# A Mamba scan kernel: the carried state of slot 10 joined one slot ahead, the first dt loaded in slot 27, the gate z copied one half a slot

## The chip, the cores and the metric

The kernel runs on one core of one Trainium2 chip. The metric is the device time of one execution in microseconds (us). Three runs of the kernel before gave 4239.77, 4239.93 and 4242.26 us; the median, 4239.93 us, is the time before.

## The reference, cut to what matters

The program computes two layers of a hybrid of convolution, attention and Mamba on 4096 tokens of 256 channels, and then a mixture of two experts. The change lies in the Mamba stage alone. That stage computes, for each of two directions (forward, and backward over the reversed tokens):

```
xc, z = split(in_proj(x));  xc = silu(conv4(xc));  dt, B, C = x_proj(xc);  dt = softplus(dt_proj(dt))
h[t] = exp(dt[t] * A) * h[t-1] + dt[t] * B[t] * xc[t]        # 512 channels x 16 states
y[t] = sum over states (h[t] * C[t]) + xc[t] * Dp;   out = out_proj(y * silu(z))
```

Both directions are added, normalised, put through a small two-layer network and added to the input.

## The kernel before, in words

Four stages follow each other: convolutions with depthwise taps, attention, the Mamba stage (mamba_phase), and the experts. All tensors are float32.

The Mamba stage works in 16 chunks, numbered i: 8 blocks of 512 tokens, with the two directions taken in turn (d = i % 2). A chunk has 4 channel groups e, 4 state groups k and 2 halves j of a group: 32 slots, numbered at = 8 e + 2 k + j/2. One slot is one scan instruction on VectorE (DVE) over 128 lanes and 2 x 512 elements. A lane is a pair of channel and state, and two runs of 512 tokens stand side by side in one instruction. For a slot n these steps exist, each of them on a fixed engine:

- decay(n), ScalarE (ACT), line L1667: two exponentials that make the factors da in PSUM. Two such PSUM tiles exist.
- inflow(n), GpSimd (POOL), L1677: the product dbx of the loaded row dtxr with the row b. Three dbx tiles exist.
- bring(n), ACT, L1708: adds the state carried over from the chunk before into the first element of the second run, in dbx. It exists from chunk 2 on, and it needs inflow(n) and the tile brought.
- recur(n), DVE: the scan, L1688, and in 27 of 32 slots the product with the row c, L1693. In slots 4, 10, 12, 18 and 28 (POOLED) that product is made by POOL, L1698.
- keep(n), ACT, L1716: stores the end of the scan as the state.
- sum_states, TensorE (PE), L1723 and L1725: sums over states into y. close (DVE, L1733) multiplies y with the gate z.

The order of the instructions on each engine is the order of the loop body; each engine runs its own list in that order and waits where a value is missing. In slot n the body issues: carry (if this slot has one), inflow(n+2), keep(n-1), decay(n+1), bring(n+1), recur(n), the loads for later slots, sum_states, and then one step of each generator that runs beside the scan: prepare (the projections, convolution and dt of chunk i+1), from slot 27 on also the prepare of chunk i+2, and tail (the small network of a finished block), whose pieces are held back in slots where the named engine is full.

The steps of prepare(q) fall into fixed slots of chunk q-1: the Silu of xc (L1301, with a load of ACT's function table ahead of it and another behind it, for the next exponential) in slot 8, the projection by wx (PE, L1306) in slot 9, the Ln (L1346) in slot 23, and the last six steps in slots 24 to 29. In those six, dt_piece adds the softplus on POOL (L1370), takes the first dt of every row (L1375) and writes it to DRAM (first_row, L1378, by the SP queue, one for each pair of channel groups), or writes the dt rows themselves (dtd, L1385). load_first (L1391, SP) reads first_row back, spread over the 128 lanes, as first_r. The z part (L1251 on PE, two products at a time in the two PSUM tiles "mm"; L1362 on ACT, the copies into z) lies there too.

The tile brought is made by carry in three parts: POOL multiplies first_r with A (L1401), ACT takes the exponential (L1403), and POOL multiplies with the old state (L1406). For channel groups 0 and 1 of the next chunk (h = 0) part 0 is issued at the start of slot 30, part 1 at the end of slot 30, part 2 at the start of slot 31. For groups 2 and 3 (h = 1) this is done in slots 9, 10 and 11 of the chunk itself, with load_first in slot 1.

All loads and stores of the stage go through one queue, SP, in the order of the code: besides the above the rows b and c (L1414), dtr and dtxr (L1424; the two for slots 0 and 1 are issued in slots 27 and 29 of the chunk before), and u (L1260). An SP instruction that must wait holds everything behind it. Its transfers take eight completion semaphores in turn.

Of the kernel before, what the change touches and what calls it, by code (L numbers as in the profile page):

```python
# [14 lines left out]
FP = mybir.dt.float32  # L15
# [9 lines left out]
P = 128  # L25
# [4 lines left out]
N = 512  # L30
# [1137 lines left out]
def mamba_phase(cx, early, w_in, w_x, w_out, w1, w2, x1d, ud, bcd, dtd, x2d, u2d, usum):  # L1168
# [11 lines left out]
    nc, tc = cx.nc, cx.tc  # L1180
    with ExitStack() as ctx:
# [87 lines left out]
        def prepare(q):  # L1269

            d, got = q % 2, gots[q]

            ps = in_pair(q, 0)
            yield
            yield
            xp = early.wide("xp")
            nc.scalar.copy(xp[:, :, 0:3], halo[d])
            for v in range(2):
                nc.scalar.copy(xp[:, v, 3:], ps[v])
            ps = in_pair(q, 2)  # L1280
            yield
            yield
            for v in range(2):
                nc.scalar.copy(xp[:, 2 + v, 3:], ps[v])
            nc.scalar.copy(halo[d], xp[:, :, N : N + 3])
            for _ in range(4):
                yield

            xc = None
            for e in range(ET + 1):  # L1290
                if e > 0:
                    xc = got["xc"] = xc or pr.tile([P, ET, N], FP, name="xc", tag="xc")
                    nc.scalar.activation(xc[:, e - 1, :], ps, AF.Identity, bias=cx.col(f"convb{d}", e - 1))
                if e < ET:
                    ps = mm_psum()
                    for k in range(4):
                        nc.tensor.matmul(  # L1297
                            ps, taps[d][:, 4 * e + k, :], xp[:, e, k : k + N], start=k == 0, stop=k == 3
                        )
                yield  # L1300
            nc.scalar.activation(xc, xc, AF.Silu)  # L1301
            yield
            ps = mm_psum()
            nx = DR + 2 * DS
            for e in range(ET):
                nc.tensor.matmul(ps[0:nx, :], wx[d][:, e, :], xc[:, e, :], start=e == 0, stop=e == ET - 1)  # L1306
            yield
            xd = few()[0:nx, :]
            nc.scalar.copy(xd, ps[0:nx, :])

            at = 0 if d else DR
            nc.sync.dma_start(out=bcd[q], in_=xd[at : at + 2 * DS, :])
            yield


            r = slice(32 * d, 32 * d + DR)
            ex = dt = None
            for e in range(ET + 1):
                if e > 0:
                    ex = early.wide("ex")[:, :, 0:N] if e == 1 else ex  # L1320
                    dt = dt or sp.tile([P, ET, N], FP, name="dt", tag="dt")
                    nc.scalar.activation(ex[:, e - 1, :], ps, AF.Abs, bias=cx.col(f"dtb{d}", e - 1))
                    nc.scalar.activation(dt[:, e - 1, :], ps, AF.Relu, bias=cx.col(f"dtb{d}", e - 1))
                if e < ET:
                    ps = mm_psum()
                    nc.tensor.matmul(ps, wdt[r, P * e : P * e + P], xd[r, :], start=True, stop=True)
                yield

            nc.scalar.activation(ex, ex, AF.Exp, scale=-1.0)
            yield  # L1330
            rds, sums = {}, {}
            for e in range(ET + 2):
                if e < ET:
                    rd = rds[e] = few()
                    nc.scalar.activation(rd, ex[:, e, :], AF.Identity, scale=-1.0, bias=-1.0)
                    nc.scalar.add(rd, rd, 1.0)
                if e > 1:
                    nc.scalar.copy(dt[:, e - 2, :], sums.pop(e - 2))
                if 0 < e <= ET:
                    ps = sums[e - 1] = mm_psum()  # L1340
                    for v, x in enumerate((rds.pop(e - 1), ex[:, e - 1, :], dt[:, e - 1, :])):
                        nc.tensor.matmul(ps, cx.ident, x, start=v == 0, stop=v == 2)
                yield


            nc.scalar.activation(ex, ex, AF.Ln, bias=1.0)  # L1346
            zs = in_pair(q, ET)
            yield
            got["dt"] = dt
            for at, (v, e) in enumerate(((0, 0), (1, 0), (0, 1), (0, 2), (0, 3), (1, 1))):  # L1350
                dt_piece(q, v, e, ex)
                if at == 4 and q > 1:
                    load_first(q, 0)
                if at == 1:
                    zs = in_pair(q, ET + 2)
                    if q + 1 < 2 * NCH:
                        load_u(q + 1)
                if at in (0, 2):
                    z = sp.tile([P, 2, N], FP, name="z", tag="z", bufs=3)
                    got.setdefault("z", []).append(z)  # L1360
                    for f in range(2):
                        nc.scalar.copy(z[:, f, :], zs[f])  # L1362
                yield

        def dt_piece(q, v, e, ex=None, eng=nc.gpsimd):
# [387 lines left out]
        with tc.manual_schedule(engines=ORDERED):  # L1753
            gots[0] = {"u": early.u}
            begin = start()
            step(begin)
            coming = prepare(1)
            tails, prep, out, ending = [], None, None, None
            for n, (i, e, k, j) in enumerate(slots):
                at = n % SPS  # L1760
                if at == 0:
                    prep, coming = coming, None
                if at in CARRY and 1 < i + (at > 16) < 2 * NCH:
                    carry(i + (at > 16), *CARRY[at])
                inflow(n + 2)
                if n > 0:
                    keep(n - 1)
                if n > 0:
                    decay(n + 1)
                bring(n + 1)  # L1770
                if at == 8:
                    bring(n + 2)
                recur(n)
                nxt = (i, e + 1) if e < ET - 1 else (i + 1, 0)
                if nxt[0] < 2 * NCH:
                    if e == ET - 1 and j == 0:
                        load_bc(i + 1, k)
                    if (k, j) == (1, 2):
                        load_dt(*nxt, 0)
                    if (k, j) == (2, 2):  # L1780
                        load_dt(*nxt, 2)
                if n > 0 and (n - 1) % SPS in POOLED:
                    pooled(n - 1)
                if j == 2 and n > 2 and (n - 3) % SPS in POOLED:
                    sum_states(n - 3)
                if j == 0 and n > 0:
                    if (n - 2) % SPS not in POOLED:
                        sum_states(n - 2)
                    if k == 0:
                        close(*slots[n - 2][:2])  # L1790
                        if e == 0:
                            out = output(i - 1)
                if 1 <= at <= 3 and out is not None:
                    step(out)
                    if at == 3:
                        out = None
                        if (i - 1) % 2:
                            tails.append(tail((i - 1) // 2))
                if at == 0 and i > 0:
                    for z in gots[i]["z"]:  # L1800
                        nc.scalar.activation(z, z, AF.Silu)
                if i == 0:
                    step(begin)
                step(prep, LATE.get(at, 1) if i == 0 else 1)
                if at >= SPS - AHEAD and i + 2 < 2 * NCH:
                    coming = coming or prepare(i + 2)
                    step(coming)
                if i > 0 and at in (2, 4):
                    dt_piece(i, 1, 2 if at == 2 else 3)
                if at == 1 and i > 1:  # L1810
                    load_first(i, 1)
                elif at in (10, 30) and 1 < i + (at > 16) < 2 * NCH:
                    carry(i + (at > 16), at < 16, 1)
                if i == 2 * NCH - 1 and at in (26, 28):
                    ending = ending or last_output()
                    step(ending)
                if tails and (i == 2 * NCH - 1 or at not in FULL[needs[0]]):
                    needs[0] = next(tails[0], None)
                    if needs[0] is None:
                        tails.pop(0)  # L1820
                        needs[0] = "PE"
            sum_states(len(slots) - 2)
            close(2 * NCH - 1, ET - 1)
            for t in tails:
                drain(t)
            drain(ending)
            last_tail(NCH - 1)
# [324 lines left out]
```

## Time and profile before

| what | value |
|---|---|
| median of three runs | 4239.93 us |
| the profiled execution: its own time | 4233.11 us |
| its span, first to last instruction | 4231.3 us |
| convolutions and attention, start of span to 2016 us: DVE busy | 1644.6 of 2016 us |
| Mamba, chunks 0 and 1, 2016 to 2254 us: DVE busy | 216.8 of 238 us |
| Mamba, chunks 2 to 15, 2254 to 3910 us: DVE, ACT, POOL, PE busy | 1575.1, 1267.0, 1422.4, 1342.1 of 1656 us |
| end of Mamba and experts, 3910 to 4231 us: PE busy | 278.3 of 321 us |
| granted TensorE clock, share of full | 0.918 |

A row of the groups names the line, the engine, the operation, the tiles written and read, the count, the busy time and mean duration, and after the second bar the idle time just before such instructions with what ended it. A row of the waits names who waited for whom, the time in total, how often, and the longest. A row of the timeline names the start, the duration, the engine, the line, and in brackets the idle time before. In the tables of waits a wait is put down to the semaphore that came last by the profile, so a name can be that of a neighbour on the same engine.

### The profile page before, as it was taken

The page shows a single profiled execution, that of the slowest core. Times are in us where ns is not written, and L with a number is a line of the kernel's source. Part 1 is how long each engine was busy: PE and PEld are TensorE (multiplying, and loading weights), DVE is VectorE, ACT ScalarE, POOL GpSimd, SP SyncE. Part 2 cuts the span into 40 slices and gives each one's busy share as a digit, 9 for nine tenths or more (in the row PEclk, how much of TensorE's full clock was granted, in tenths as well). Part 3 has the DMA queues.
Part 4 walks back from the last instruction along what each step waited for, and adds up shares of the span by engine and source line. Part 5 has one row for each costly group of instructions (what it writes and reads, how often), then busy time and mean ns, then how long its engine had stood idle before and what let it go on. Part 6 is the DMA issues. An engine that isn't in the chain of part 4 may idle for free. (4 is left out here: it accounts for less than half of the span.)

```text
span 4231.3 us, 43479 instructions
## 1 busy us (share of the span) xinstructions
PE 3603.2 (85%) x15080; PEld 1175.6 (28%) x15080; DVE 3503.0 (83%) x2898; ACT 2675.6 (63%) x4176; POOL 1740.9 (41%) x1132
## 2 busy tenths in 40 slices
PE   4769894999999999999788888878888888875798
PEld 2324341222222222222222222222222222321343
DVE  6997876888888888778899999999999999999211
ACT  1111224888788788777777778777787777774122
POOL 2210000000000000000888889888888888897000
PEclk9889996999999999999888999989899898977899
DMA  4422224000000000002333443433334433432121
GB/s 160 138 77 92 75 75 133 4 28 15 21 26 11 24 24 15 17 14 74 115 125 113 130 117 123 126 115 123 115 108 125 130 124 116 133 117 73 65 65 39
DMA packets 150531, 351.18 MB, mean 83 GB/s; under 512 B 35493, under 2 KB 44453, under 8 KB 150046
## 3 DMA queue, kind: packets, MB, share of 16 engines
q1 hardware_dynamic: 139214, 313.17, 23.4%
q0 software_dynamic: 11088, 35.14, 2.4%
q8 instruction: 120, 1.97, 0.2%
q14 instruction: 109, 0.89, 0.1%
HBM read 268.69 MB, written 79.56 MB: 82 GB/s over the span
## 5 line engine op out<-in xcount | busy, mean ns | idle before, releaser
L1677 POOL TENSOR_TENSOR dbx<-dtxr,b 128x1024 f32<-128x1024 f32 x512 | 1203.0, 2361 | 201.9 <-DVE da L1688 106.0
L961 ACT ACTIVATE e<-sc 128x1024 f32<-128x1024 f32 x1024 | 992.6, 1023 | 201.4 <-PE sc L954 160.3
L1688 DVE TENSOR_TENSOR_SCAN da<-da,state,dbx 128x1024 f32<-128x1024 f32 x432 | 1014.3, 2348 | 40.4 <-ACT state L1716 19.3
L882 DVE TENSOR_TENSOR s<-s,e 128x1024 f32<-128x1024 f32 x768 | 880.8, 1218 | 45.4 <-ACT e L961 44.9
L1667 ACT ACTIVATE da<-dtr,aneg 128x512 f32<-128x512 f32 x1024 | 708.0, 691 | 32.8 <-DMA dtr<-dtd 2.9
L954 PE MATMUL sc<-q,kS 32*128 32x512 f32 x4096 | 653.6, 643 | 19.5 <-DMA kS<-kd 13.0
L132 POOL TENSOR_TENSOR ln_few<-ln_few,minus_half 128x4 f32<-128x4 f32 x29 | 29.5, 1016 | 1414.2 <-DMA ln_few<-ln_row 1414.2
L1693 DVE TENSOR_TENSOR h<-da,c 128x1024 f32<-128x1024 f32 x432 | 529.2, 1225 | 32.6 <-DVE da L1688 0.4
L889 PE MATMUL av<-e,vT 128*32 128x512 f32 x4096 | 548.9, 607 | 3.7 <-ACT o L895 3.7
L452 PE MATMUL cv<-v,u 128*128 128x512 f32 x928 | 420.7, 614 | 58.8 <-DVE pad L272 21.2
L1725 PE MATMUL y<-h,sel 128*32 128x512 f32 x2048 | 378.7, 655 | 101.3 <-DVE h L1693 83.9
L954 PEld LDWEIGHTS sc<-q,kS 32*128 32x128 f32 x4096 | 211.6, 183 | 465.5 <-issue 244.3
L1251 PE MATMUL mm<-u,win 128*128 128x512 f32 x496 | 255.4, 663 | 80.9 <-ACT z L1362 34.3
L452 PEld LDWEIGHTS cv<-v,u 128*128 128x128 f32 x928 | 181.1, 197 | 294.6 <-issue 241.3
L528 DVE SCALAR_TENSOR_TENSOR acc<-pad,wdw_s,acc 128x768 f32<-128x768 f32 (+1 forms) x192 | 244.6, 1279 | 19.0 <-ACT acc L524 13.3
L1716 ACT COPY state<-da 128x2 f32<-128x2 f32 x431 | 68.1, 158 | 257.9 <-DVE h L1693 256.8
L1297 PE MATMUL mm<-xp,taps 128*128 128x512 f32 x480 | 213.6, 597 | 3.5 <-DVE m L1446 3.4
L882 DVE TENSOR_TENSOR s<-e 128x1024 f32<-128x1024 f32 x128 | 150.9, 1220 | 72.8 <-ACT e L961 72.6
L1688 DVE TENSOR_TENSOR_SCAN h<-da,state,dbx 128x1024 f32<-128x1024 f32 x80 | 187.5, 2343 | 16.5 <-ACT state L1716 7.0
L889 PEld LDWEIGHTS av<-e,vT 128*32 128x32 f32 x4096 | 81.3, 108 | 395.9 <-issue 378.3
L1698 POOL TENSOR_TENSOR h<-h,c 128x1024 f32<-128x1024 f32 x80 | 188.6, 2358 | 2.1 <-ACT state L1716 2.1
L1251 PEld LDWEIGHTS mm<-u,win 128*128 128x128 f32 x496 | 100.9, 212 | 236.5 <-issue 105.1
(347 smaller groups left out, 3821.3 us busy)
## 6 DMA issues: line engine op xcount, KB each, us to landing
dtr<-dtd SPq DMA_DIRECT2D x128, 512.0 KB
dtxr<-dtd SPq DMA_DIRECT2D x128, 512.0 KB
b<-bcd SPq DMA_DIRECT2D x64, 256.0 KB
c<-bcd SPq DMA_DIRECT2D x64, 256.0 KB
dtd<-dt SPq DMA_DIRECT2D x64, 256.0 KB
dtd<-few SPq DMA_DIRECT2D x64, 256.0 KB
u<-uv SPq DMA_DIRECT2D x24, 640.0 KB
u<-ud SPq DMA_DIRECT2D x16, 512.0 KB
```

The source lines that it names most:

```text
L452: nc.tensor.matmul(rows4(ps), u[:, dy, P * ci : P * ci + P], v[:, dy : dy + HR, ci, :], start=dy + ci == 0, stop=dy == k - 1 and ci == CT - 1,
L528: nc.vector.scalar_tensor_tensor(o, src, w_ap, o, ALU.mult, ALU.add)
L882: nc.vector.tensor_tensor(z, x, y, ALU.add)
L889: nc.tensor.matmul(g.av[32 * h : 32 * h + 32, :], vT[:, kb, P * t + 32 * h : P * t + 32 * h + 32], es[h // 2][:, h % 2, :], start=kb == 0, ...
L954: nc.tensor.matmul(ps[h // 2][:, h % 2, :], kS[r, t, P * kb : P * kb + P], q_t[r, t, :], start=True, stop=True,)
L961: nc.scalar.activation(e, ps[i], AF.Exp)
L1251: nc.tensor.matmul(ps, win[d][:, t, P * e : P * e + P], u[:, t, ::-1] if d else u[:, t, :], start=t == 0, stop=t == CT - 1,)
L1667: nc.scalar.activation(da[:, v, :], dts[i, e, j][0][:, v, :], AF.Exp, scale=aneg[i % 2][:, a : a + 1])
L1677: nc.gpsimd.tensor_tensor(u, dts[i, e, j][1], bcs[i, k][0][:, None, :].to_broadcast([P, 2, N]), ALU.mult)
L1688: nc.vector.tensor_tensor_scan(das[n].rearrange("p v n -> p (v n)"), da.rearrange("p v n -> p (v n)"), u.rearrange("p v n -> p (v n)"), st ...
L1693: nc.vector.tensor_tensor(h, da, bcs[i, k][1][:, None, :].to_broadcast([P, 2, N]), ALU.mult)
L1725: nc.tensor.matmul(ys[i, e][32 * j : 32 * j + 32, :], cx.sel, hs[n + j // 2][:, j % 2, :], start=False, stop=k == SQ - 1,)
```

## The change

In slot 8 the body issued bring(9) and, at once behind it, bring(10); it now issues bring(9) alone, and bring(10) follows decay(10) in slot 9 as for every other slot. load_first(q, 0) moves from behind dt_piece(q, 0, 3) in slot 28 to ahead of dt_piece(q, 0, 2) in slot 27. The four z copies, made two at a time in slots 24 and 26, are now made one each in slots 24, 25, 26 and 27; the one in slot 25 stands ahead of the second pair of z projections. No instruction is added or dropped. The orders of POOL, PE and DVE stay as they were.

```diff
             for at, (v, e) in enumerate(((0, 0), (1, 0), (0, 1), (0, 2), (0, 3), (1, 1))):
+                if at == 3 and q > 1:
+                    load_first(q, 0)
                 dt_piece(q, v, e, ex)
-                if at == 4 and q > 1:
-                    load_first(q, 0)
+                if at in (0, 2):
+                    z = sp.tile([P, 2, N], FP, name="z", tag="z", bufs=3)
+                    got.setdefault("z", []).append(z)
+                if at < 4:
+                    nc.scalar.copy(z[:, at % 2, :], zs[at % 2])
                 if at == 1:
                     zs = in_pair(q, ET + 2)
                     if q + 1 < 2 * NCH:
                         load_u(q + 1)
-                if at in (0, 2):
-                    z = sp.tile([P, 2, N], FP, name="z", tag="z", bufs=3)
-                    got.setdefault("z", []).append(z)
-                    for f in range(2):
-                        nc.scalar.copy(z[:, f, :], zs[f])
                 yield
...
                 bring(n + 1)
-                if at == 8:
-                    bring(n + 2)
                 recur(n)
```

## The prediction

> **What bounds the kernel now.** I read the stages' busy times first: only Mamba is touched, and in chunks 2 to 15 DVE is busy 1575 of 1656 us (95%). The groups then say what DVE does there, and the waits say who stops it.
>
> ```profile
> L1688 DVE TENSOR_TENSOR_SCAN da<-da,state,dbx 128x1024 f32<-128x1024 f32 x432 | 1014.3, 2348 | 40.4 <-ACT state L1716 19.3
> ```
>
> With the product of L1693 (1.23 us, below) a slot costs 3.58 us of DVE. The change touches none of that, so it can only win or lose DVE's idle time. The waits of DVE in chunks 2 to 15, then those of ACT:
>
> ```profile
> DVE da L1688 <- ACT state L1716: 17.7, 21, 2.0
> DVE da L1688 <- ACT dbx L1708: 12.7, 15, 3.1
> ```
> ```profile
> ACT brought L1403 <- POOL brought L1401: 29.6, 13, 4.5
> ACT dbx L1708 <- POOL dbx L1677: 20.9, 21, 2.0
> ```
>
> DVE waits for ACT, and ACT waits for POOL at just the instructions that the change moves. By slot (the scans of the timeline numbered 0 to 511; a stall is the idle time before a scan over the -0.08 us that scans show back to back) the stalls of over 0.1 us in chunks 2 to 15 lie at slot 0 (9.8 us in sum), slot 2 (15.6), slot 10 (16.2), 25 (2.9) and 26 (3.9), with a few single ones at slots 12 and 13; all other scans follow without a gap.
>
> Slot 10 in chunk 5, ACT's timeline, then DVE's:
>
> ```profile
> 2638.08 0.28 ACT L1708 ACTIVATE dbx<-dbx,brought 128x1 f32<-128x1 f32 x1
> 2639.15 0.29 ACT L1708 ACTIVATE dbx<-dbx,brought 128x1 f32<-128x1 f32 x1 [0.79 <-POOL dbx L1677]
> 2639.45 1.28 ACT L1301 ACT_TABLE_LOAD   x1
> 2640.74 1.91 ACT L1301 ACTIVATE xc<-xc 128x2048 f32<-128x2048 f32 x1
> ...
> 2644.01 1.42 ACT L1667 ACTIVATE da<-dtr,aneg 128x512 f32<-128x512 f32 x2
> ```
> ```profile
> 2642.99 1.23 DVE L1693 TENSOR_TENSOR h<-da,c 128x1024 f32<-128x1024 f32 x1
> 2645.53 2.35 DVE L1688 TENSOR_TENSOR_SCAN h<-da,state,dbx 128x1024 f32<-128x1024 f32 x1 [1.32 <-ACT da L1667]
> ```
>
> ACT stands idle for inflow(10); behind that wait are queued Silu and both table loads, then decay(10), which ends 0.10 us before scan 10 starts. That wait is on the path.
>
> [...] The trace has 16 landing marks for a first_row, up to 4.7 us from first to last. [...] load_first must wait on SP for the last mark of first_row. In the trace, first_r into chunk 2 is issued 0.07 us after that mark.
>
> **bring(10).** In slot 8 it costs ACT its wait (0.79 us in chunk 5) and 0.28 us. In slot 9, inflow(10) is long done (2639.11), so it costs 0.28 us behind decay(10), of which 0.14 shows (decay end to scan is 0.24 us where a bring stands between, 0.10 here). Nothing else holds Silu: its input is ACT's own, and keep(8) and decay(10) need DVE results of 2638.76 and 2640.09. So scan 10 gains the smaller of its stall and wait + 0.14. Waits of ACT by chunk: 0.66, 1.52, 0.79, 1.52, 0.41, 1.50, 1.44, 1.51, 0.75, 2.01, 0.87, 1.51 in chunks 3 to 14; in 2 and 15 none, and no stall. Stalls: 1.27, 1.00, 1.40, 1.00, 1.16, 1.33, 2.05, 0.99, 1.35, 2.12, 1.48, 1.00. Sum of the smaller ones: 13.2 us. What is late next? wx on PE follows Silu and comes earlier too; inflow(13) has over 2 us. I take -13.0; the ends are -9 (0.3 us lost in each) and -16 (all stalls).
>
> **First dt.** SP into chunk 6, and the POOL step that needs it:
>
> ```profile
> 2709.00 0.55 SPq L1378 DMA_DIRECT2D first_row<-first  x1
> ...
> 2710.86 0.60 SPq L1414 DMA_DIRECT2D b<-bcd  x1
> 2713.31 0.51 SPq L1414 DMA_DIRECT2D c<-bcd  x1
> 2715.91 0.33 SPq L1378 DMA_DIRECT2D first_row<-first  x1
> 2716.33 0.72 SPq L1391 DMA_DIRECT2D first_r<-first_row  x1
> ```
> ```profile
> 2723.56 0.22 POOL L1401 TENSOR_TENSOR brought<-aneg,first_r 128x16 f32<-128x16 f32 x1 [1.57 <-DMA dtxr<-dtd]
> ```
>
> The releaser named is a neighbour: first_r's last mark is at 2723.49. The new place is behind the first dtxr, issued at 2710.26 in this list, but first_row lands at 2715.17, so the issue is near 2715.2, 1.1 us earlier; what counts is that b and c, 512 KB, then lie behind it: I expect the landing near dtxr's, 2718.5. POOL is ready at 2721.99, so the whole wait on L1401 goes, in 8 of 14 boundaries by over 0.1 us (3.35, 2.73, 1.37, 0.24, 1.57, 2.71, 1.90, 2.37). Slot 0's stall goes with it. But slot 2 of the next chunk is late next: its bring(1) needs inflow(1), and that needs the second dtxr, whose landing (2725.95) is set by the same transfers, only reordered. From bring(1) to scan 2 are 6.6 us of Silu, two table loads and decay. With x for the shift of that landing, scan 2 gains, into chunks 2 to 7, 11 and 13: 0.93, 0.96, 0.04, 0.05, 0.80, 0.71, 0.25, 0.32, each less x; 4.1 us at x = 0, and chunk 14 loses x as well: 9x. Behind SP's new wait stand b, c, first_row and dtr/dtxr, issued up to 1.2 us later than now (into chunk 4), though that still is over 7 us ahead of their landing. The trace doesn't show this order. Ends for x: -0.5 (fewer early loads compete) and 1.2 us (the issue delay shows fully); I take 0.3[...]. So -4.1 + 2.7 = -1.4; ends -8 and +6.5.
>
> **z.** In the seven even chunks from 2 on scan 26 stalls 0.55 us behind this ACT queue:
>
> ```profile
> 2583.03 1.05 ACT L1362 COPY z<-mm 128x512 f32<-128x512 f32 x2
> 2583.97 1.52 ACT L1457 ACTIVATE hn<-hn,small 128x512 f32<-128x512 f32 x2
> ...
> 2585.57 1.42 ACT L1667 ACTIVATE da<-dtr,aneg 128x512 f32<-128x512 f32 x2
> ```
>
> One copy fewer ahead (1.05 - 0.57 = 0.48 us) ends it: 7 x 0.48 = 3.4 us. The added wait is PE's: the second product of slot 25 waits for the copy behind bring(26), up to 0.4 us, with u's load behind it on SP and all of the above behind that. Where the landing sets slot 2 the 0.48 is lost again, which leaves about two of seven: -1.0; ends -3.8 and +2. In odd chunks bring(26) has over 4 us before scan 26: nothing, covered by scan 25 and a tail step.
>
> **Sum.** -13.0 - 1.4 - 1.0 = -15.4 us. Against the profiled execution: 4233.1 - 15.4 = 4217.7. That execution lay 6.8 us under the median of the runs; on the median, 4239.9 - 15.4 = 4224.5.
>
> **Rivals.** (1) Given back: slot 10 gains, but x is 1.2 and PE's wait costs 2 us: -13 + 6.5 + 2 = -4.5, 4235.4. For it: DVE-bound stretches end at slot 2, where the landing decides; against it: the landings come over 7 us after issue. (2) Slower: SP, blocked on first_row, leaves the DMA engines dry, so that the second dtxr lands 3 us later. Then nine boundaries lose 27 - 4 and the others, whose slack is 0.9 to 3.5 us, some 5 more: +28 - 13 = +15, 4254.9. It decides from x = 1.8 on. For it: first_row lands 6 to 8 us after its issue in the busy boundaries. Against: dtr and dtxr, 1 MB, are still moving when first_row lands. (3) No effect: what is freed at slot 10 is waited for at slots 11 to 13, by PE's wx or POOL: 4239. For it: chunk 15 stalls 1.1 us at slot 12. Against: ACT's whole queue moves up with Silu, so its exponential and POOL's part 2 do too.
>
> **Chances.** Forecast 0.70 (4216 to 4231), rival 1 0.17, rival 2 0.08, rival 3 0.05. A difference under 0.2% (8.5 us) can't be told from none: rivals 1 and 3 lie within. Of the forecast 0.02 ends there too, and of rival 1 0.06 passes 4231.5: faster 0.74, same 0.18, slower 0.08. The range, 4215 to 4238, leaves out rival 2, part of 3, and a gain of over 25 us.
>
> **What would show it.** Right: ACT has no idle time ahead of Silu in slot 8, scan 10's stalls sum to about 3 us, L1403's wait for L1401 falls from 29.6 to under 18, scan 0 hardly stalls. Slot 2's stalls grow, from 15.6 towards 15.6 + 9.8 - 1.4 = 24 us, since slot 0's move there; slot 26's vanish. Wrong: L1677's wait for dtxr at slot 1 grows by more than 1 us a boundary, or new stalls stand at slots 11 to 13.

## The result, and the profile after

Eleven runs of the changed kernel against eleven of the kernel before give a ratio of 0.9968, 95% interval 0.9958 to 0.9977: 0.32% faster, 13.6 us of 4241 (9.8 to 17.8). The medians are 4228.28 and 4241.35 us. The profiled execution of the kernel after took 4228.78 us with a span of 4227.0 us. One execution says less than the ratio: its scans began at 2020.5 us, those of the execution before at 2016.5 us, though the stages ahead of them are the same in both. So the stalls are compared slot by slot, and the sizes are taken from the ratios.

The waits of DVE in chunks 2 to 15, then those of ACT (who waited for whom: us in total, times, longest):

```profile
DVE da L1688 <- ACT state L1716: 22.3, 14, 2.7
DVE xc L1733 <- PE y L1725: 13.3, 7, 2.8
DVE da L1688 <- ACT dbx L1708: 7.5, 11, 2.0
DVE h L1688 <- ACT dbx L1708: 2.5, 6, 0.5
```
```profile
ACT dbx L1708 <- POOL dbx L1677: 18.7, 14, 3.3
ACT brought L1403 <- POOL brought L1401: 16.1, 13, 2.1
```

The fourth line is slot 10, now released by the bring itself, 0.4 us each in six odd chunks. ACT's wait for L1401 fell from 29.6 to 16.1 us, but its wait for the products dbx hardly fell (20.9 to 18.7): in slot 10 it went (14.5 us before, none after), and at the chunk boundary it came back (bring(1): 1.1 us before, 16.0 after). Slot 10 of chunk 5, ACT's timeline, then DVE's:

```profile
2639.45 0.28 ACT L1708 ACTIVATE dbx<-dbx,brought 128x1 f32<-128x1 f32 x1
2639.75 1.28 ACT L1301 ACT_TABLE_LOAD   x1
...
2644.31 1.42 ACT L1667 ACTIVATE da<-dtr,aneg 128x512 f32<-128x512 f32 x2
2645.67 0.28 ACT L1708 ACTIVATE dbx<-dbx,brought 128x1 f32<-128x1 f32 x1
```
```profile
2644.36 1.23 DVE L1693 TENSOR_TENSOR h<-da,c 128x1024 f32<-128x1024 f32 x1
2645.98 2.35 DVE L1688 TENSOR_TENSOR_SCAN h<-da,state,dbx 128x1024 f32<-128x1024 f32 x1 [0.40 <-ACT dbx L1708]
```

The table load for Silu follows bring(9) at once (bring(9) ends at 2639.73, the load starts at 2639.75), and bring(10) stands behind decay(10), 0.28 us long. The stall before scan 10 fell from 1.32 to 0.40 us.

The boundary into chunk 6, SP's issues, then POOL:

```profile
2710.70 0.55 SPq L1424 DMA_DIRECT2D dtxr<-dtd  x1
2715.16 0.51 SPq L1391 DMA_DIRECT2D first_r<-first_row  x1
2715.72 0.60 SPq L1414 DMA_DIRECT2D b<-bcd  x1
2716.41 0.55 SPq L1414 DMA_DIRECT2D c<-bcd  x1
2717.06 0.54 SPq L1378 DMA_DIRECT2D first_row<-first  x1
2717.69 0.51 SPq L1424 DMA_DIRECT2D dtr<-dtd  x1
```
```profile
2722.25 0.19 POOL L1383 TENSOR_TENSOR dt<-dt,odd 128x1 f32<-128x1 f32 x1
2722.39 0.22 POOL L1401 TENSOR_TENSOR brought<-aneg,first_r 128x16 f32<-128x16 f32 x1
```

SP stands still for 3.91 us, from 2711.25 to 2715.16, until first_row has landed: its last of 16 landing marks is at 2715.14, and into each of the 14 chunks first_r goes out 0.02 us after that mark. The rows b and c, which before went out at 2710.86 and 2713.31, now follow behind it. POOL's L1401 no longer waits. Into chunk 3 the wait appears two instructions later (POOL, then DVE):

```profile
2369.21 0.22 POOL L1406 TENSOR_TENSOR brought<-brought,state 128x16 f32<-128x16 f32 x1
2374.70 9.29 POOL L1677 TENSOR_TENSOR dbx<-dtxr,b 128x1024 f32<-128x1024 f32 x4 [5.27 <-DMA dtxr<-dtd]
```
```profile
2377.40 2.36 DVE L1688 TENSOR_TENSOR_SCAN da<-da,state,dbx 128x1024 f32<-128x1024 f32 x1 [2.01 <-ACT dbx L1708]
2379.80 1.22 DVE L1693 TENSOR_TENSOR h<-da,c 128x1024 f32<-128x1024 f32 x1
2383.71 2.36 DVE L1688 TENSOR_TENSOR_SCAN da<-da,state,dbx 128x1024 f32<-128x1024 f32 x1 [2.69 <-ACT state L1716]
```

inflow(1) waits 5.27 us for the second dtxr, and scans 1 and 2 stall by 2.01 and 2.69 us behind it.

The stalls of every profile, summed over chunks 2 to 15 from the timelines (a scan's idle time over the -0.08 us of scans back to back), are below. "L1401" and "inflow(1)" are POOL's waits at the 14 boundaries; "landing" is the mean time from the start of scan 31 to the last mark of the second dtxr. All in us; each row is one execution.

| kernel | slot 0 | slot 1 | slot 2 | slot 10 | slot 26 | L1401 | inflow(1) | landing |
|---|---|---|---|---|---|---|---|---|
| before | 9.8 | 0.0 | 15.6 | 16.2 | 3.8 | 16.3 | 3.4 | 2.97 |
| after | 0.0 | 5.6 | 23.5 | 3.0 | 0.5 | 0.0 | 26.7 | 3.80 |
| bring alone | 12.7 | 0.8 | 21.1 | 3.0 | 3.9 | 21.4 | 11.2 | 3.91 |
| first dt alone | 0.0 | 4.6 | 24.9 | 15.3 | 3.8 | 0.0 | 28.7 | 3.73 |
| z alone | 17.5 | 0.0 | 18.3 | 16.4 | 0.5 | 24.5 | 5.4 | 3.86 |
| bring, z | 13.8 | 0.1 | 18.2 | 3.0 | 0.5 | 19.6 | 4.5 | 3.49 |
| bring, z, first dt ahead of the second row | 8.7 | 0.0 | 21.1 | 3.0 | 0.5 | 17.1 | 10.0 | 3.63 |
| after, with b and c late | 0.0 | 1.1 | 16.1 | 3.0 | 0.5 | 0.0 | 12.1 | 2.33 |
| bring, first dt, b and c late | 0.0 | 0.0 | 11.8 | 3.0 | 3.9 | 0.0 | 7.4 | 1.79 |
| bring, z, b and c late | 0.1 | 0.0 | 12.0 | 3.0 | 0.5 | 1.4 | 0.4 | 1.58 |
| bring, z, b and c late, again | 0.6 | 0.0 | 11.4 | 3.0 | 0.5 | 0.0 | 2.8 | 1.42 |
| bring, b and c late | 0.0 | 0.0 | 9.5 | 3.0 | 3.9 | 0.0 | 2.5 | 1.42 |

### The profile page after: what moved, and what is told of

Its sections match the earlier page's. It is cut to its first block, busy times and chain, and to the rows that moved or that the text cites. A ratio compares the mean times of both kernels' runs of the same rounds, so it can differ in the third digit from the quotient of the medians.

```text
span 4227.0 us, 43473 instructions
## 1 busy us (share of the span) xinstructions
PE 3618.8 (86%) x15080; PEld 1177.9 (28%) x15080; DVE 3501.6 (83%) x2898; ACT 2673.7 (63%) x4176; POOL 1739.2 (41%) x1132
## 5 line engine op out<-in xcount | busy, mean ns | idle before, releaser
L1677 POOL TENSOR_TENSOR dbx<-dtxr,b 128x1024 f32<-128x1024 f32 x512 | 1202.1, 2359 | 231.2 <-DVE da L1688 116.4
L1667 ACT ACTIVATE da<-dtr,aneg 128x512 f32<-128x512 f32 x1024 | 708.1, 692 | 34.6 <-DMA dtr<-dtd 4.7
L954 PE MATMUL sc<-q,kS 32*128 32x512 f32 x4096 | 655.3, 644 | 21.1 <-DMA kS<-kd 11.9
L1725 PE MATMUL y<-h,sel 128*32 128x512 f32 x2048 | 379.6, 660 | 98.4 <-DVE h L1693 80.6
L528 DVE SCALAR_TENSOR_TENSOR acc<-pad,wdw_s,acc 128x768 f32<-128x768 f32 (+1 forms) x192 | 244.6, 1279 | 19.1 <-ACT acc L524 13.3
L1725 PEld LDWEIGHTS y<-h,sel 128*32 128x32 f32 x2048 | 56.9, 114 | 394.6 <-DVE h L1693 185.8
```

What stands on the lines that cost most here:

```text
L528: nc.vector.scalar_tensor_tensor(o, src, w_ap, o, ALU.mult, ALU.add)
L954: nc.tensor.matmul(ps[h // 2][:, h % 2, :], kS[r, t, P * kb : P * kb + P], q_t[r, t, :], start=True, stop=True,)
L1667: nc.scalar.activation(da[:, v, :], dts[i, e, j][0][:, v, :], AF.Exp, scale=aneg[i % 2][:, a : a + 1])
L1677: nc.gpsimd.tensor_tensor(u, dts[i, e, j][1], bcs[i, k][0][:, None, :].to_broadcast([P, 2, N]), ALU.mult)
L1725: nc.tensor.matmul(ys[i, e][32 * j : 32 * j + 32, :], cx.sel, hs[n + j // 2][:, j % 2, :], start=False, stop=k == SQ - 1,)
```

## The experiments

The theory is that of the prediction: the wait in slot 10 was on the path, and the stall at slot 0 moves on to slots 1 and 2, where the landing of the second dtxr decides. The ratios are to the kernel before, with 95% intervals; a thousandth is 4.2 us.

**Each part alone.** The bring alone:

```diff
                 bring(n + 1)
-                if at == 8:
-                    bring(n + 2)
```

> Only the bring of slot 10 is moved to slot 9. Theory (the wait of ScalarE for inflow(10) was on the path): the stalls before scan 10 fall from 16.2 us to about 3 us and nothing takes their place, so about -13 us, ratio 0.9969. Rival (what is freed at slot 10 is waited for at slots 11 to 13, and the full change won through the earlier first dt): within 3 us of before, ratio 0.9993 to 1.0007.

Measured: 0.9970 (0.9961 to 0.9979), -12.7 us. Its waits of DVE:

```profile
DVE da L1688 <- ACT state L1716: 23.2, 21, 2.7
...
DVE h L1688 <- ACT dbx L1708: 2.5, 6, 0.5
```

Slot 10 is down to 3.0 us as in the full change. The rival falls: at slots 11 to 13 nothing takes its place (slot 12 has one stall of 1.25 us, which it had before, and slot 13 none).

The first dt alone:

```diff
+                if at == 3 and q > 1:
+                    load_first(q, 0)
                 dt_piece(q, v, e, ex)
-                if at == 4 and q > 1:
-                    load_first(q, 0)
```

> Only load_first is moved to slot 27. Theory (the stall of slot 0 moves to slots 1 and 2, where the second dtxr decides): slot 0 loses its stall of about 10 us, slots 1 and 2 gain as much or up to 4 us more; the time is within -2 and +4 us of before, ratio 0.9995 to 1.0010. Rival (the wait of GpSimd for first_r was on the path): -8 us or more, ratio 0.998. Second rival (the blocked SP queue starves the DMA engines): +10 us or more.

Measured: 0.9994 (0.9986 to 1.0002), -2.5 us (-5.9 to +0.8), which can't be told from nothing. Slot 0's stall is gone, and slots 1 and 2 hold 29.5 us instead of 15.6. Both rivals fall: a gain of 8 us lies outside the interval, and so does a loss of 10.

z alone:

```diff
+                if at in (0, 2):
+                    z = sp.tile([P, 2, N], FP, name="z", tag="z", bufs=3)
+                    got.setdefault("z", []).append(z)
+                if at < 4:
+                    nc.scalar.copy(z[:, at % 2, :], zs[at % 2])
                 if at == 1:
...
-                if at in (0, 2):
-                    z = sp.tile([P, 2, N], FP, name="z", tag="z", bufs=3)
-                    got.setdefault("z", []).append(z)
-                    for f in range(2):
-                        nc.scalar.copy(z[:, f, :], zs[f])
```

> Only the z copies are spread. Theory: the stall before scan 26 of even chunks goes (-3.4 us), part of it is lost again at slot 2: -1 to -3.4 us, ratio 0.9992 to 0.9998. Rival (TensorE, which now waits for the copy behind bring(26), hands its delay on through the load of u, or y comes later in slot 24): 0 to +5 us, ratio 1.000 to 1.0012.

Measured: 1.0004 (0.9997 to 1.0012), +1.7 us. Scan 26 did lose 3.3 us of stall (3.8 to 0.5), and the time shows none of it: the rival's side, though the interval reaches to -1.3 us.

**Bring and z, without the first dt.** Against the full change, load_first goes back to slot 28:

```diff
-                if at == 3 and q > 1:
-                    load_first(q, 0)
                 dt_piece(q, v, e, ex)
+                if at == 4 and q > 1:
+                    load_first(q, 0)
```

> The full change without the move of load_first. Theory: -14 to -16 us, ratio about 0.9964, as good as the full change or up to 3 us better, since the move of load_first brings nothing. Rival (the earlier first dt is worth its 4 us or more): 4 us or more slower than the full change, -9 us at best.

Measured: 0.9972 (0.9961 to 0.9983), -11.9 us, which the full change's interval overlaps. Slots 0 to 2 hold 32.1 us here and 29.1 in the full change. It is less than the theory's 14 to 16 us, and the rival's 4 us are not excluded by the ratio. Both estimates of what the first dt is worth, 1.7 us here and 2.5 us alone, are too small to be told from nothing.

**load_first without the blocked queue.** Against the full change, in slot 28, ahead of the dt_piece that writes the second first_row:

```diff
-                if at == 3 and q > 1:
+                if at == 4 and q > 1:
                     load_first(q, 0)
                 dt_piece(q, v, e, ex)
```

> The full change with load_first in slot 28, ahead of dt_piece(q, 0, 3): behind b and c, but not behind the second first_row. Theory: SP isn't blocked, first_r lands 0.5 to 1 us earlier than before, so slot 0 keeps about two thirds of its stall, and slot 2 is as before: within 3 us of the full change, ratio 0.997. Rival (the blocked SP queue in slot 27 costs the full change time): 5 us or more faster than the full change.

Measured: 0.9968 (0.9957 to 0.9979), as the full change. Slot 0 keeps 8.7 us, slot 2 holds 21.1: 29.8 us in sum, against 29.1. SP's stop in slot 27 cost the full change nothing that can be told.

**What decides slot 2.** The rows b and c of the next chunk's third state group, 512 KB, are issued behind dtr and dtxr of slot 29. inflow(4), which POOL is given in slot 2 of that chunk, is the first to read them:

```diff
-                    if e == ET - 1 and j == 0:
+                    if e == ET - 1 and j == 0 and k != 2:
                         load_bc(i + 1, k)
...
                         load_dt(*nxt, 2)
+                        if e == ET - 1:
+                            load_bc(i + 1, k)
```

On the full change:

> The full change, and the rows b and c of the third state group of the next chunk (512 KB, needed in its slot 4) are issued behind dtr and dtxr of slot 29 instead of in slot 28. Theory (the landing of the second dtxr decides slot 2): it lands about 3 us earlier, the stalls of slots 0 to 2 fall from 29 us to about 8 us (14 x 0.58, what Silu and the table loads cost anyway), so about -20 us against the full change, ratio 0.992. Rival (slot 2 is set by ScalarE's Silu of z and its table loads alone, whatever lands when): as the full change, 0.9968 within 0.001.

Measured: 0.9935 (0.9920 to 0.9950), -27.5 us, 14 us faster than the full change. The landing comes 1.5 us earlier, not 3, and slots 0 to 2 hold 17.2 us instead of 29.1. The rival falls: Silu and the table loads were the same, and of the 21.0 us of stall above what they cost anyway (14 x 0.58 = 8.1, an estimate from slot 2 of the kernel before, which stalls 0.57 or 0.58 us in six of its 14 chunks) 11.9 went. No stall appears at slots 3 to 9, so the late rows come in time. The theory's size was too large: 20 us were expected.

The same edit on bring and z, with load_first in its old place:

> The same order of b and c, without the move of load_first. Theory: first_r then lands about 3 us earlier too, since it is no longer behind those rows, so the wait of GpSimd for it nearly goes and the time is within 3 us of the run with load_first moved, ratio 0.992 to 0.993. Rival (only the early first dt can clear slot 0): 8 us or more slower than that run.

Measured: 0.9927 (0.9912 to 0.9943), -31 us, the same as the run on the full change within the intervals. The wait of L1401 is 1.4 us in all. No gain of the early first dt is seen once b and c are out of its way.

The same edit on bring and the move of load_first, with z copied two at a time. Against the run on the full change:

```diff
-                if at in (0, 2):
-                    z = sp.tile([P, 2, N], FP, name="z", tag="z", bufs=3)
-                    got.setdefault("z", []).append(z)
-                if at < 4:
-                    nc.scalar.copy(z[:, at % 2, :], zs[at % 2])
...
+                if at in (0, 2):
+                    z = sp.tile([P, 2, N], FP, name="z", tag="z", bufs=3)
+                    got.setdefault("z", []).append(z)
+                    for f in range(2):
+                        nc.scalar.copy(z[:, f, :], zs[f])
```

> The run with b and c behind dtr and dtxr, with the z copies two at a time as before. Theory (z's 3.4 us are real at scan 26 and were lost at slot 2 to the landing): where the landing no longer decides, they show: 3.4 us slower than that run with z spread, at the edge of what can be told, and the stall before scan 26 is 3.8 us in its profile. Rival (spreading z costs as much elsewhere): the same time or faster.

Measured: 0.9941 (0.9927 to 0.9955), against 0.9935: inconclusive.

**z once more, and the best version.** Bring and late rows alone, and the run with z spread again beside it. The first is, against the kernel before:

```diff
                 bring(n + 1)
-                if at == 8:
-                    bring(n + 2)
                 recur(n)
...
-                    if e == ET - 1 and j == 0:
+                    if e == ET - 1 and j == 0 and k != 2:
                         load_bc(i + 1, k)
...
                         load_dt(*nxt, 2)
+                        if e == ET - 1:
+                            load_bc(i + 1, k)
```

> The move of bring(10) and the late b and c, without the moves of load_first and of z. Theory (z's gain at scan 26 is real where the landing no longer decides slot 2): 2 to 4 us slower than the same kernel with z spread, with 3.8 us of stall before scan 26. Rival (spreading z costs as much elsewhere): as that kernel or faster. Both: about ratio 0.993, since bring and the order of b and c carry the gain.

> The kernel with bring moved, z spread and b and c late, timed again beside the run without z: ratio 0.9927 within 0.0015, and 2 to 4 us faster than that run by the theory, the same by the rival.

Measured: 0.9911 (0.9898 to 0.9925) without z and 0.9914 (0.9900 to 0.9928) with it, medians 4204.99 and 4205.32 us: -38 and -36 us, more than the 0.993 that was expected of both. The six runs with z are 2.0 us slower in the mean than the six without (-1.8 to +5.9), so a gain of 3.4 us by z is excluded here. DVE of the two at slots 25 and 26 of chunk 4, without z, then with it:

```profile
2569.46 2.36 DVE L1688 TENSOR_TENSOR_SCAN da<-da,state,dbx 128x1024 f32<-128x1024 f32 x1 [0.33 <-ACT dbx L1708]
2571.85 1.23 DVE L1693 TENSOR_TENSOR h<-da,c 128x1024 f32<-128x1024 f32 x1
2573.54 2.36 DVE L1688 TENSOR_TENSOR_SCAN da<-da,state,dbx 128x1024 f32<-128x1024 f32 x1 [0.47 <-ACT state L1716]
```
```profile
2575.14 1.22 DVE L1693 TENSOR_TENSOR h<-da,c 128x1024 f32<-128x1024 f32 x1
2576.34 2.36 DVE L1688 TENSOR_TENSOR_SCAN da<-da,state,dbx 128x1024 f32<-128x1024 f32 x1
```

The stall before scan 26 (the last line of each view) is there in the one and not in the other, and the times can't be told apart. In these profiles slots 0 to 2 hold 9.5 us without z and 12.0 and 12.1 with it, and DVE's wait for L1725 is 7.1 us without and 8.7 and 8.9 with it, which together is more than the 3.4 us; but rows of the table whose kernels do not differ at the boundary (before, bring alone) differ by 9 us in slots 0 to 2, so this is a hint and no more. The theory that z pays where the landing doesn't decide is not borne out.

Bring with the late rows, 0.89% under the kernel before, is the simplest of the versions that can't be told from the best: one call taken out and one pair of loads moved. Against the bring alone (0.9970) the late rows are worth some 25 us, and the stalls of slots 0 to 2 in the two profiles differ by as much (34.6 and 9.5 us). The late rows without the bring were not run. What SP issues there into chunk 6, with the old place of load_first:

```profile
2694.69 0.55 SPq L1424 DMA_DIRECT2D dtxr<-dtd  x1
2700.52 0.33 SPq L1378 DMA_DIRECT2D first_row<-first  x1
2700.89 0.51 SPq L1391 DMA_DIRECT2D first_r<-first_row  x1
2701.73 0.51 SPq L1424 DMA_DIRECT2D dtr<-dtd  x1
2702.29 0.60 SPq L1424 DMA_DIRECT2D dtxr<-dtd  x1
2702.94 0.60 SPq L1414 DMA_DIRECT2D b<-bcd  x1
```

first_r is issued where it was and still meets no wait on POOL.

## Why the prediction was right, and where it was not

- **bring(10).** Forecast -13.0 us from the smaller of stall and wait, chunk by chunk; measured alone -12.7 (-16.5 to -8.9), and slot 10 fell by 16.2 - 3.0 = 13.2 us in the profile, the very sum. The left-over sits where it was expected: in six odd chunks, whose stall was larger than ACT's wait, 0.47 to 0.63 us each.
- **First dt.** Forecast -1.4; measured alone -2.5 (-5.9 to +0.8), so its size is neither confirmed nor refuted. The mechanism held: in the full change L1401's wait of 16.3 us vanished, and POOL's wait at inflow(1) rose from 3.4 to 26.7. Slot 2's stall was to grow to 24 us and holds 23.5. That this is so near is in part luck. Not foreseen: slot 1 stalls too, 5.6 us, because a late inflow(1) holds bring(1), which scan 1 needs; only scan 2 was worked out, and slots 0 to 2 together hold 29.1 us.
- **The landing of the second dtxr.** Its shift x was taken as 0.3 us, the author's estimate, which the trace of before does not show. The two runs with the early load land at 3.80 and 3.73, the four that keep it behind b, c and the second first_row (before, bring alone, z alone, bring with z) at 3.56 in the mean: +0.2. But those four scatter from 2.97 to 3.91, so the sign of x is not shown. In these profiles the early load does go with a later issue, by some 0.5 us: counted from the start of scan 31, the second dtxr is issued at -3.54 and -3.81 us with the early load, and at -4.38 to -4.00 in the other four. The profile of before lay at the early end: its slots 0 to 2 hold 25.4 us, those of the other three 32 to 36.
- **One sign was badly chosen.** The prediction named "L1677's wait for dtxr at slot 1 grows by more than 1 us a boundary" as showing it wrong. It grew by 23.3 us over 14, 1.7 each. Of this, 16.3 us are the wait taken over from L1401, which the prediction's own move of the stall from slot 0 to slot 2 implies. The other 7.0 us go with a landing that is 0.83 us later in this profile than in that of before, within the scatter above. The sign should have been the landing time, over several profiles.
- **z.** Forecast -1.0, with 3.4 us gained at scan 26 and two thirds lost at the landing. The 3.4 us were there; none of it reached the time: +1.7 alone (-1.3 to +5.1), 0.9914 against 0.9911 with late rows. The forecast lies in the interval, but the step "where the landing sets slot 2 the 0.48 is lost again" is not the whole story, since with the landing mostly out of the way it doesn't show either. Where it is lost is open.
- **Sum.** -15.4 was forecast; the ratio says -13.6, and the parts alone sum to -13.5. The bring carries it. The other two parts were forecast at 2.4 us together, less than these runs can tell from nothing, and z missed by 2.7 us in one direction where the first dt missed by 1.1 in the other: that the sum came out near says nothing for these two.
- **Rivals.** Given back (-4.5) lies outside the interval; the first dt alone, at most +0.8 us, leaves by the prediction's own sum (-4.1 + 9x) no x over 0.54, where this rival took 1.2. Slower falls: SP's stop was seen, 3.91 us long into chunk 6, but the second dtxr didn't land 3 us later, and load_first without that stop gave the same time. No effect falls with the run of the bring alone.

## What to carry to other kernels

On an engine that takes its list in order, price a wait by what is queued behind it: a 0.28 us instruction that waited 0.4 to 2 us ahead of two table loads cost 13 us over 12 chunks; behind them it no longer waited, and 3 us of the stall were left. When a stall at one place goes, ask at once what is late one and two steps later; here the same queue of transfers held the next product, and of the changes tried at this boundary only taking 512 KB from ahead of it gained time that can be told. Move what isn't needed soon behind what is, before bringing anything forward.

## What the runs showed that was not expected

- The same transfers in the same order land 2.5 us apart in different executions (the second dtxr into chunk 3, counted from the start of scan 31: at 4.85 us in the profile of before, 6.08 with the bring alone, 7.34 with z alone). Part of that is a later issue; from its own issue this transfer took 8.31, 8.94 and 10.20 us, and the one into chunk 10 took 6.42, 10.47 and 7.57. One profile is too little to size a DMA wait.
- TensorE's eight products of L1481 in slot 23 of odd chunks took 3.7 us from first start to last end in some executions and 5.4 in others. Chunk 9 of the kernel after:

```profile
3158.36 3.32 PE L1481 MATMUL tl<-a1a,w2s 128*128 128x512 f32 x4 [2.49 <-DVE m L1486]
3161.47 2.28 PE L1481 MATMUL tl<-a1b,w2s 128*128 128x512 f32 x4
```

In chunk 5 of the kernel before the same two groups take 1.98 and 1.88 us after the same idle time of 2.49 us. The granted clock differs. The first view is of the kernel after, around these products, the second of the kernel before, over the products of chunk 5 (the clock stands ahead of the DMA share):

```profile
3155.45:3158.86 3.41, 0.92 (x5) 0.30 (x2) 3.31 (x4) 2.05 (x6) 0.66 (x1) 1.00 0.98 337
3158.86:3162.27 3.41, 3.41 (x5) 1.35 (x4) 3.31 (x3) 3.38 (x4) 3.30 (x2) 0.50 0.04 11
3162.27:3165.68 3.41, 3.41 (x9) 1.52 (x8) 2.95 (x2) 3.35 (x7) 3.33 (x4) 1.00 0.01 2
```
```profile
2692.03:2695.73 3.70, 3.70 (x9) 1.79 (x10) 3.60 (x3) 3.64 (x5) 3.42 (x2) 1.00 0.16 60
```

The products of before run at 1.00 throughout; those of after fall to 0.50 for 3.41 us, half a microsecond after they began, and then return to 1.00. In the profiles of before and after every change of the clock (173 and 187 of them) lies within 0.001 us of a grid with a step of 3.413 us. Counted from the start of the span the two grids are 0.016 us apart, so the two executions differ in when the products come, not in the grid. Of the 72 such groups in chunks 3 to 13 of the twelve profiles, 39 follow the idle time of 2.49 us. In the 13 slow ones at least 2.00 us of it fell within one step of the grid (all 2.49 us in chunk 9 of after), in the 26 fast ones at most 1.93 us (1.71 us in chunk 5 of before). The other 33 follow 1.0 us or less and are all fast. So the same kernel is slow or fast here by where that idle time lies on the grid in that execution; what makes the clock fall is not shown.

The slower products hold the y that close waits for: DVE's wait for L1725 behind them is 2.41 or 2.76 us in the 13 slow cases and 0.71 to 1.07 in the others. In chunks 2 to 15 that wait is 13.3 us after and 7.3 before, 7.5 to 12.7 in the other six profiles with the spread copies and 7.1 to 9.9 in the other four without. Whether the spread copies make the 2.49 us more frequent is not settled.
